# A graph layer on one core: kept messages, three slot tables, gather rows by ScalarE, and a rearranged start and end

## The chip, the cores and the metric

The kernel runs on one core of one Trainium2 chip. The metric is the device time of one execution in microseconds (us); beside it stands one execution recorded by the hardware profiler, with a span from its first to its last instruction. The core has TensorE (PE, matrix products), VectorE (DVE), ScalarE (ACT), GpSimd (POOL) and SyncE (SP), which here only starts DMA transfers. Each engine takes its instructions in order, so an instruction that waits holds up all that is queued behind it on its engine.

## The reference, cut to what matters

```python
# x [12500,128]; 400000 edges, sorted by dst; src random; src is the row that is added to
h   = relu(layernorm(x)) @ W_in2f.T
Wij = (smu(edge_attr_20 @ W_f1.T + b_f1) @ W_f2.T + b_f2) * edge_weight[:, None]
agg = segment_sum(h[dst] * Wij, src, 12500)          # rows gathered at dst, summed at src
out = x + (smu(agg @ W_o1.T + b_o1) @ W_o2.T + b_o2)
# smu(x) = ((1+a)x + (1-a) x erf(mu (1-a) x)) / 2, written as a gelu plus a linear part
```

## The kernel before, in words

Edges are taken in tiles of 128; four tiles are a group (782 groups, the unit of the main loop) and two groups a supergroup (391). The sum over `src`, which is in random order, is made by sorting messages into bins. A bin is 128 nodes (98 bins). A run of supergroups is an epoch, and each epoch has a table `buf{k}` in DRAM with a fixed number of slots for each bin. A message takes the next free slot of its bin: POOL writes it there with one scatter, an indirect DMA of 128 rows of 129 numbers, for every tile (L649). When an epoch is over, its table is read back bin by bin and added up on TensorE while the next epoch's messages are made.

One group goes through these steps; the numbers are lines of the profile:

- `load` (SP): edge attributes `f` (L439), target positions `rbc` broadcast to all partitions (L449), and a window of 42 rows of h (L463);
- `hide`, `bend`, `smooth`: first filter product on TensorE (`pu`, L563), gelu on ScalarE (L571), linear part on VectorE (L579);
- `pick`: 0/1 gather rows `oh` by VectorE, once for a supergroup (L472);
- `gather`, `take`: rows of h by a product with `oh` (`ph`, L597), copied by ScalarE (L605);
- `weigh`, `mix`: second filter product (`pw`, L616), times the gathered rows on VectorE (`mt`, L626);
- `bins`, `count`, `read`, `number`: the slot of every message (VectorE L497, TensorE L511 to L514, VectorE L541 and L550);
- `turn`: the message times w_o1, which also turns edges onto partitions (`pt`, TensorE, L636);
- `send`: ScalarE scales by the edge weight into an `ms` tile (L643, L646), and POOL scatters it.

The steps of several groups are interleaved by hand; each engine gets its instructions in the order of the program. POOL's scatters come only from `send`, and there are six `ms` tiles, so that ScalarE can be at most six groups ahead of POOL. The main loop is, in its order (before.py, L938 to L958):

```python
            if g:
                turn(g)
                send(g)
            ...
            number(g + 1); weigh(g + 1); gather(g + 1); take(g + 1)
            parts(k - 1, lo + (hi - lo) // 2)      # half of this group's adds
            mix(g + 1)
            ...
            hide(g + 2); bend(g + 2); count(g + 2); smooth(g + 2)
            if g % PER == 0:
                pick((g + 4) // PER)
            bins(g + 3)
            read(g + 2)
            parts(k - 1, hi)                       # the other half
```

`parts` adds up the epoch before: `fetch` reads table rows on SP's queue (L680), `choose` makes 0/1 rows by comparing each row's node number (L691, VectorE), `add` multiplies both on TensorE into `pg` (L704), and VectorE adds `pg` into `agg` (L717, L715 for the first epoch). `begin` and the first `choose` of an epoch stand in its second and third group: they wait for the last scatter of the epoch before, and VectorE waits with them.

Tables are cleared with zeros beforehand by DMAs on SP's queue (`clear`, L179), as slots stay empty. In the first epoch the rows of h are made between the steps (`rows_of_h`: L205 normalizes on ScalarE). Near the end of the last epoch rows of x come in for the output (`old_rows`), and POOL adds the output bias to them (`with_bias`, L250). After the last scatter, the last table is added up, and for every four bins gelu (L994, ScalarE), a sum (L1000, POOL), the product with w_o2 (L264) and the store follow.

At the very start POOL fills four buffers and a block of zeros, loads weights and clears the last bin's rows, before its first scatter (L393 to L411).

Of the kernel before, what the change touches and what calls it, by code (L numbers as in the profile page):

```python
# [31 lines left out]
PARTS = (59, 59, 59, 59, 48, 37, 27, 27, 16)  # L32
# [8 lines left out]
def gnn_kernel(  # L41
# [46 lines left out]
    for a, n in eps_of:  # L88
        mean = n * SUP * P * P / N
        dev = SIGMA * math.sqrt(mean)  # L90
        CAP.append(math.ceil((mean + dev) / P) * P)
        ZMIN.append(max(0, math.floor((mean - dev) / ZP) * ZP))
# [10 lines left out]
    bufs = [dram.tile([NB * CAP[k], ROW], F32, name=f"buf{k}") for k in range(EPOCHS)]  # L103
# [17 lines left out]
    nc.vector.tensor_add(prow, prow, late)  # L121
    irow = const.tile([P, P], F32, name="irow")
# [5 lines left out]
    nc.vector.tensor_scalar(lift, ident, BIG, None, op0=ALU.mult)  # L128
    nc.vector.scalar_tensor_tensor(tri, irow, pcol, lift, op0=ALU.is_gt, op1=ALU.add)
    ones_h = const.tile([P, P], F16, name="ones_h")  # L130
    nc.vector.memset(ones_h, 1.0)
    rest_h = const.tile([P, P], F16, name="rest_h")
    nc.vector.tensor_sub(rest_h, ones_h, tri)
    none = const.tile([P, NB], F16, name="none")
    nc.vector.memset(none, 0.0)
# [6 lines left out]
    b1w = const.tile([P, P], F32, name="b1w")  # L142
# [14 lines left out]
    b2row = const.tile([1, P], F32, name="b2row")  # L157
    b1 = const.tile([P, 1], F32, name="b1")
    bz = const.tile([P, 1], F32, name="bz")
    w_o1 = const.tile([P, P], F32, name="w_o1")  # L160
# [4 lines left out]
    zero = const.tile([ZP, CB * max(c - z for c, z in zip(CAP, ZMIN)) * ROW // ZP], F32, name="zero")  # L165
# [69 lines left out]
    units = [(b, n, P) for b, n in chunks(NB - 1, GRP)] + [(NB - 1, 1, LASTB)]  # L235
# [39 lines left out]
    with tc.tile_pool(name="ld", bufs=4) as ld, \  # L275
# [8 lines left out]
        irow_ps = ps1.tile([P, GRP * P], F32, name="irow_ps")[:, 0:P]  # L284
        nc.vector.tensor_copy(irow_ps, irow)
# [106 lines left out]
        fill(0, nc.vector)  # L392
        nc.gpsimd.memset(w_f1, 0.0)  # L393
        nc.gpsimd.dma_start(w_f1[0:R, :], w_f1_t)
        nc.gpsimd.dma_start(w_f1[R:R + 1, :], b_f1)
        nc.sync.dma_start(fbufs[0][0:R, :], f_t[:, 0:SUP * P])
        nc.scalar.dma_start(w_o1, w_o1_t)
        nc.scalar.dma_start(x_sb[:, 1:HEAD, :], bin_rows(x, 1, HEAD - 1))
        nc.gpsimd.dma_start(w_f2, w_f2_t)
        nc.gpsimd.dma_start(b2, b_f2.rearrange("o p -> p o"))  # L400
        one["fetched"]()
        nc.gpsimd.dma_start(w_sb[:, 0:CH], w_col[:, 0:CH])
        fill(1, nc.gpsimd)
        nc.gpsimd.memset(zero, 0.0)
# [390 lines left out]
        for s in (1, 2):  # L795
            load(s)
# [397 lines left out]
```

## Time and profile before

| | |
|---|---|
| time, median of 3 runs | 4111.01 us (4106.05 to 4113.0) |
| the profiled execution: time; span | 4114.52 us; 4112.7 us |
| mean granted TensorE clock | 0.976 |
| busy: TensorE, VectorE, ScalarE, POOL | 3675.1, 3450.5, 1944.9, 3096.4 us |
| DMA | 820.83 MB, mean 200 GB/s |
| chain that ended last, by engine | PE 39%, DVE 29%, DMA 18%, ACT 6%, issue 5%, POOL 2% |

How to read it: a row of a group shows line, engine, operation, output and inputs with the count, then busy time and mean duration of one in ns, then the engine's idle time just before them and what ended most of it. "Issue" is idle time in which the engine waited for nothing that the profile shows. Rows of the timeline start with the start and duration in us. Rows of the windows begin with the stretch and its length, then busy time and count of the engines in the order PE, PEld (weight loads), DVE, ACT, POOL (or of the one engine asked for), then granted clock, DMA share and GB/s. A TensorE product in float32 shows as two passes, a transpose as one.

### The profile page before, as it was taken

What the parts mean: (1) busy time and instruction counts of PE and PEld (TensorE: products, weight loads), DVE (VectorE), ACT (ScalarE), POOL (GpSimd) and SP (SyncE); (2) the same over time, 40 slices, a digit from 0 to 9 for tenths busy, and PEclk for the clock granted to TensorE, in tenths of its full rate; (3) what the DMA queues carried; (4) which work ended last, traced back from release to release, by engine and by line L of the source; (5) the groups of instructions that cost most, each with busy time, mean ns of one, the idle gap of its engine ahead of it and who ended that gap; (6) DMA issues with size and microseconds to landing.
All of it is one profiled execution on the core that took longest, in us unless ns stands there. A gap on an engine that the chain in (4) does not pass through costs nothing.

```text
span 4112.7 us, 74065 instructions
## 1 busy us (share of the span) xinstructions
PE 3675.1 (89%) x21113; PEld 2552.3 (62%) x21117; DVE 3450.5 (84%) x7657; ACT 1944.9 (47%) x5690; POOL 3096.4 (75%) x3199
## 2 busy tenths in 40 slices
PE   7878887999888998979999979999899989999898
PEld 4445545666655666646666656666677767666678
DVE  8988776888878888868888868888799979888897
ACT  4457754444444444435444434444444434444442
POOL 6777777777777777777777777777777777777775
PEclk9999998999999999989999989999999999999999
DMA  6866656766647666646766647777688789887668
GB/s 187 231 187 182 191 166 183 213 202 195 188 141 219 198 201 197 199 146 196 212 199 187 199 148 207 210 204 211 176 228 223 195 230 242 221 228 221 176 195 248
DMA packets 564245, 820.83 MB, mean 200 GB/s; under 512 B 178033, under 2 KB 378488, under 8 KB 563698
## 3 DMA queue, kind: packets, MB, share of 16 engines
q1 hardware_dynamic: 456096, 604.98, 53.5%
q0 software_dynamic: 100320, 207.40, 15.7%
q10 hardware_dynamic: 7410, 3.65, 0.3%
q8 instruction: 167, 2.74, 0.3%
q14 instruction: 252, 2.06, 0.2%
HBM read 442.34 MB, written 373.37 MB: 198 GB/s over the span
## 4 chain that ended last, share of the span: by engine, by line
PE 39%; DVE 29%; DMA 18%; ACT 6%; issue 5%; POOL 2%; DVEq 0%; ACTq 0%; POOLq 0%; SPq 0%
DMA buf<-ms,ix 17%; PE pt L636 11%; PE pg L704 9%; PE pw L616 8%; DVE se L691 8%; PE pu L563 7%; DVE mt L626 5%; DVE so L497 5%; DVE sm L579 3%; DVE sl L541 3%; ACT ge L571 2%; ACT ms L646 2%; PE ph L597 2%; POOL buf L649 2%; DVE agg L717 1%
## 5 line engine op out<-in xcount | busy, mean ns | idle before, releaser
L649 POOL DMA_INDIRECT buf<-ms,ix x3125 | 3025.4, 968 | 972.7 <-issue 395.9
L646 ACT ACTIVATE ms<-pt,w_sb 128x128 f32<-128x128 f32 x3125 | 888.8, 368 | 1125.5 <-PE pt L636 1118.0
L636 PE MATMUL pt<-w_o,mt 128*128 128x128 f32 x6250 | 881.3, 284 | 390.9 <-DVE mt L626 388.4
L704 PEld LDWEIGHTS pg<-se,rw 128*128 128x128 f32 x8036 | 1052.4, 192 | 249.7 <-issue 210.8
L704 PE MATMUL pg<-se,rw 128*128 128x128 f32 x8036 | 1148.8, 280 | 4.5 <-DVE se L691 3.7
L636 PEld LDWEIGHTS pt<-w_o,mt 128*128 128x128 f32 x6250 | 765.5, 193 | 478.7 <-DVE mt L626 474.5
L497 DVE SCALAR_TENSOR_TENSOR so<-irow_ps,hi_f,so 128x98 f16<-128x98 f32 x3116 | 989.0, 317 | 82.7
L616 PE MATMUL pw<-sm,w_f 128*128 128x512 f32 x1564 | 826.7, 611 | 10.4 <-DVE sm L579 8.5
L563 PE MATMUL pu<-f,w_f 128*128 128x512 f32 x1564 | 811.4, 601 | 0.0
L626 DVE SCALAR_TENSOR_TENSOR mt<-pw,b,hg 128x512 f32<-128x512 f32 x782 | 583.6, 746 | 207.3 <-ACT hg L605 203.8
L571 ACT ACTIVATE ge<-pu 128x512 f32<-128x512 f32 x782 | 468.6, 599 | 532.7 <-PE pu L563 526.5
L579 DVE SCALAR_TENSOR_TENSOR sm<-pu,ge 128x512 f32<-128x512 f32 x782 | 535.3, 684 | 187.8 <-ACT ge L571 182.0
L691 DVE TENSOR_TENSOR se<-irow_ps,rw 128x1536 f32<-128x1536 f32 (+1 forms) x345 | 587.9, 1704 | 114.3 <-DMA rw<-buf 110.2
L605 ACT ACTIVATE hg<-ph 128x512 f32<-128x512 f32 x782 | 468.6, 599 | 62.1 <-PE ph L597 44.9
L541 DVE TENSOR_REDUCE sl<-pc 128x4 f32<-128x392 f32 x782 | 434.7, 556 | 0.0
L643 ACT ACTIVATE ms<-lo_b 128x4 f32<-128x4 bf16 x782 | 159.9, 204 | 358.7 <-DMA buf<-ms,ix 358.2
L597 PE MATMUL ph<-oh,hw 126*128 126x512 bf16 x770 | 298.3, 387 | 0.0
L563 PEld LDWEIGHTS pu<-f,w_f 128*128 128x128 f32 x1564 | 253.5, 196 | 53.4 <-issue 43.8
L511 PE MATMUL pc<-so,tri 128*128 128x392 f16 x782 | 257.9, 330 | 1.0 <-DVE sl L541 0.8
L616 PEld LDWEIGHTS pw<-sm,w_f 128*128 128x128 f32 x1564 | 241.1, 195 | 24.7 <-DVE sm L579 21.4
L513 PEld LDWEIGHTS <-rest_h 128*128 128x128 f16 x781 | 76.5, 98 | 265.9 <-issue 265.9
L513 PE MATMUL pc<-so,rest_h 128*128 128x294 f16 x781 | 225.1, 288 | 0.0
(161 smaller groups left out, 1391.0 us busy)
## 6 DMA issues: line engine op xcount, KB each, us to landing
rw<-buf SPq DMA_DIRECT2D x292, 774.0 KB
rbc<-rel_dram SPq DMA_DIRECT2D x389, 256.0 KB
buf<-zero SPq DMA_DIRECT2D x243, 387.0 KB
buf<-ms,ix POOLq DMA_INDIRECT x3125
buf<-zero SPq DMA_DIRECT2D x193, 258.0 KB
rw<-buf SPq DMA_DIRECT2D x49, 645.0 KB
f<-in_f_t SPq DMA_DIRECT2D x390, 80.0 KB
hw<-h_dram SPq DMA_DIRECT2D x770, 31.5 KB
```

The costliest lines, as they stand in the source:

```text
L497: nc.vector.scalar_tensor_tensor(so[:, j], irow_ps[:, :NB], hi_f[:, t + j:t + j + 1], so[:, j - 1] if j else before, op0=ALU.is_equal, op1 ...
L541: nc.vector.tensor_reduce(sl[:, :n], pc[:, :n], op=ALU.max, axis=AX.X)
L563: nc.tensor.matmul(pu[:, :n], w_f1, loaded[g // PER][0][:, o:o + n], start=True, stop=True)
L571: nc.scalar.activation(ge[:, :n], units_of[g][:, :n], AF.Gelu, scale=ZS)
L579: nc.vector.scalar_tensor_tensor(sm[:, :n], units_of.pop(g)[:, :n], LIN, hidden[g][:, :n], op0=ALU.mult, op1=ALU.add)
L616: nc.tensor.matmul(pw[:, :n], w_f2, hidden.pop(g)[:, :n], start=True, stop=True)
L626: nc.vector.scalar_tensor_tensor(mt[:, :n], pws.pop(g)[:, :n], b2, rows_of.pop(g)[:, :n], op0=ALU.add, op1=ALU.mult)
L636: nc.tensor.matmul(pt[:, j, :], mt[:, j * P:(j + 1) * P], w_o1, start=True, stop=True)
L646: nc.scalar.activation(ms[:, j, 0:P], pt[:, j], AF.Copy, scale=w_sb[:, t + j:t + j + 1])
L649: i = nc.gpsimd.indirect_dma_start(out=bufs[k][:, :], out_offset=bass.IndirectOffsetOnAxis(ap=ix[:, j:j + 1], axis=0), in_=ms[:, j, :], in ...
L691: nc.vector.tensor_tensor(se[:, :m], irow_ps.unsqueeze(1).to_broadcast([P, m, P]), rows_in[c][:, :m, P:P + 1].to_broadcast([P, m, P]), op= ...
L704: nc.tensor.matmul(pgs[0][:, g, :], rows_in[c][:, o, 0:P], sel[c][:, o, :], start=(q == 0), stop=(q == Q[k] - 1))
```

## The change

Six edits are made together.

1. **Kept messages.** The last supergroups form two smaller epochs (16 and 7; the epochs are now 59, 59, 59, 59, 48, 37, 27, 20, 16, 7). Their 23 supergroups are computed early, one after every nine from supergroup 67 on; their messages go to DRAM and are read back and scattered after all others, while the adds of the epochs before go on.
2. **The product with w_o1** is left out of `turn` for all messages but the kept ones: `turn` is a plain transpose, and `agg` is multiplied once by w_o1 (`fold`), when the last such epoch has been added up.
3. **Three tables** serve all ten epochs in turn. A message carries its node number plus 128 for each time its table has been used, so that old rows match nothing; only the first three epochs are cleared.
4. **Gather rows by ScalarE in two passes**, relu(1 - |target - row|), a group at a time; VectorE still makes them for the first six supergroups.
5. **The start**: weight loads from SP's queue in place of POOL's; VectorE takes a second fill; POOL's other fills wait for VectorE, which touches each buffer after its first `bins`; the counting constants come later.
6. **The end**: rows of x and their bias (now on VectorE) come beside the kept scatters; the first large `choose` of the last table is made in three pieces, and the last full unit of four bins is split in two.

The core of the diff:

```diff
-PARTS = (59, 59, 59, 59, 48, 37, 27, 27, 16)
+PARTS = (59, 59, 59, 59, 48, 37, 27, 20, 16, 7)
+SENT_LAST = 2
+BUFS = 3
-    bufs = [dram.tile([NB * CAP[k], ROW], F32, name=f"buf{k}") for k in range(EPOCHS)]
+    stores = [dram.tile([NB * CAP[k], ROW], F32, name=f"buf{k}") for k in range(min(BUFS, EPOCHS))]
+    bufs = [stores[k % BUFS][0:NB * CAP[k], :] for k in range(EPOCHS)]
...
         fill(0, nc.vector)
+        fill(1, nc.vector)
...
-        nc.gpsimd.dma_start(w_f1[0:R, :], w_f1_t)
-        nc.gpsimd.dma_start(w_f1[R:R + 1, :], b_f1)
+        nc.sync.dma_start(w_f1[0:R, :], w_f1_t)
+        nc.sync.dma_start(w_f1[R:R + 1, :], b_f1)
...
+        def quiet_ends():                      # called after product(), counting_constants(), bins(0)
+            for t in (zero, fbufs[2], zr, fbufs[3], x_sb[:, NB - 1, :]):
+                nc.vector.memset(t[:, 0:2], 0.0)
+            nc.gpsimd.memset(zero, 0.0)
+            clear(0, len(cleans) - 1, nc.gpsimd)
+            fill(2, nc.gpsimd)
+            nc.gpsimd.memset(zr, 0.0)
+            nc.gpsimd.dma_start(h_dram[NB * P:N + P, :], zr[:N + P - NB * P, :])
+            fill(3, nc.gpsimd)
+            nc.gpsimd.memset(x_sb[:, NB - 1, :], 0.0)
...
+        flow, rest_of = [], list(range(EARLY, NS))      # EARLY = 368
+        start, gap = eps_of[1][0], (eps_of[5][0] - eps_of[1][0]) // (NS - EARLY)
+        for s in range(EARLY):
+            flow.append(s)
+            if s >= start and (s - start) % gap == gap - 1 and rest_of:
+                flow.append(rest_of.pop(0))
...
+        def pick_part(g):
...
+            nc.scalar.activation(oh, loaded[s][1][:, o:o + n], AF.Abs, bias=nrow)
+            nc.scalar.activation(oh, oh, AF.Relu, scale=-1.0, bias=onesb[:, 0:1])
...
         def turn(g):
...
-                nc.tensor.matmul(pt[:, j, :], mt[:, j * P:(j + 1) * P], w_o1, start=True, stop=True)
+                if s_of(g) < EARLY:
+                    nc.tensor.transpose(pt[:, j, :], mt[:, j * P:(j + 1) * P], ident)
+                else:
+                    nc.tensor.matmul(pt[:, j, :], mt[:, j * P:(j + 1) * P], w_o1, start=True, stop=True)
...
         def send(g):
...
+            m = epoch[s_of(g)] // BUFS
+            if m:
+                nc.scalar.activation(ms[:, :n, P], lo_b[:, t:t + n], AF.Identity, bias=mark[:, m:m + 1])
...
+            if s_of(g) >= EARLY:
+                nc.scalar.dma_start(kept_rows[:, t - kept_tile:t - kept_tile + n, :], ms[:, :n, :])
+                return
+            scatter(g, ms)
...
+        def fold():
+            dst = plain.pop(0)
+            w = dst.shape[1]
+            po = ps1.tile([P, GRP * P], F32, name=("pu", "ph")[len(folded) % 2])
+            nc.tensor.matmul(po[:, :w], w_o1, dst, start=True, stop=True)
+            nc.scalar.activation(dst, po[:, :w], AF.Copy)
...
-            if g % PER == 0:
-                pick((g + 4) // PER)
+            pick_part(at(p + 4))               # at(p): the group at place p of the new order
...
+        def refill(g):
+            if g < NG:
+                t, n = groups[g]
+                back[g] = msg.tile([P, GRP, ROW], F32, name="ms")
+                nc.sync.dma_start(back[g][:, :n, :], kept_rows[:, t - kept_tile:t - kept_tile + n, :])
+
+        g1 = EARLY * PER
+        for g in range(g1, g1 + 4):
+            refill(g)
+        for g in range(g1, NG):
+            refill(g + 4)
+            k = chores(g)                      # clears, begin, choose, share of the adds
+            scatter(g, back.pop(g))
+            parts(k - 1, hi)
+            if g - g1 >= 2:
+                old(g - g1 - 2)                # rows of x, SP's queue
+            biased(g - g1 - 10)                # with_bias on VectorE
```

The kept groups have no share of the adds; `LEFT`, 36 adds of the last but one table, is still kept back for the time after the last group.

More of the change, by code (lines that the diff above doesn't have):

```diff
@@ L91, in gnn_kernel @@
         CAP.append(math.ceil((mean + dev) / P) * P)
-        ZMIN.append(max(0, math.floor((mean - dev) / ZP) * ZP))
+        ZMIN.append(max(0, math.floor((mean - dev) / ZP) * ZP) if len(ZMIN) < BUFS else 0)
+    assert all(c <= CAP[k % BUFS] for k, c in enumerate(CAP)) and (EPOCHS - 1) // BUFS < GRP
     Q = [c // P for c in CAP]
```

259 lines of the change are left out of this document (157 added, 102 removed).

## The prediction

> **What bounds the kernel now.** I read the page first: busy times, then the costliest groups.
>
> ```profile
> span 4112.7 us, 74065 instructions
> PE 3675.1 (89%) x21113; PEld 2552.3 (62%) x21117; DVE 3450.5 (84%) x7657; ACT 1944.9 (47%) x5690; POOL 3096.4 (75%) x3199
> L649 POOL DMA_INDIRECT buf<-ms,ix x3125 | 3025.4, 968 | 972.7 <-issue 395.9
> ```
>
> TensorE (PE) looks like the bound and GpSimd (POOL) like an engine with a quarter to spare. But the 972.7 us that POOL stood idle before its 3125 scatters are 0.31 us each, mostly "issue": it waited for nothing. So I read POOL's own timeline.
>
> ```profile
> 19.93 1.04 POOL L649 DMA_INDIRECT buf<-ms,ix  x1 [10.27 <-ACT ms L646]
> ...
> 1499.61 0.96 POOL L649 DMA_INDIRECT buf<-ms,ix  x1 [0.30 <-issue]
> 1500.88 0.96 POOL L649 DMA_INDIRECT buf<-ms,ix  x1 [0.30 <-DVE ix L550]
> 1502.14 0.96 POOL L649 DMA_INDIRECT buf<-ms,ix  x1 [0.30 <-DMA buf<-ms,ix]
> ...
> 4022.18 0.96 POOL L649 DMA_INDIRECT buf<-ms,ix  x1 [0.30 <-issue]
> ```
>
> A scatter starts every 1.265 us (1499.61 to 1502.14, two steps), 0.96 busy and a fixed 0.30 whatever releaser is named. The 3124 steps from first to last take at least 3124 x 1.265 = 3951.9 us; they took 4022.18 - 19.93 = 4002.3. POOL is saturated from 20 to 4022 us. The span is 19.9 (head) + 3951.9 + 50.4 (excess) + 90.5 (after the last scatter). No edit here changes the number of scatters, so only head, excess and tail can shrink; time taken from TensorE or VectorE (DVE) in between buys nothing by itself.
>
> The excess: 3125 x (0.968 - 0.96) = 25 us is scatters that ran long; about 14 us is POOL's bias adds (below); some 12 us is left for scatters that came late.
>
> **The production rate.** Messages queue before POOL in six `ms` tiles. After each table change VectorE sits out POOL's whole backlog, then the engines refill the queue at their own rate:
>
> ```profile
> 641.77 1.76 DVE L691 TENSOR_TENSOR se<-irow_ps,rw 128x1536 f32<-128x1536 f32 x1 [20.46 <-DMA rw<-buf]
> 649.10:906.90 257.80, 40.33 (x54) 1.00 0.69 203
> 649.10:906.90 257.80, 242.81 (x1415) 169.67 (x1414) 226.40 (x493) 128.16 (x379) 195.97 (x204) 1.00 0.69 203
> ```
>
> The second line counts the `mt` products of L626: 54 groups in 257.8 us, 4.77 us a group against POOL's 4 x 1.265 = 5.06. The third (columns PE, PEld, DVE, ACT, POOL) gives per group TensorE 4.50, VectorE 4.19, ScalarE (ACT) 2.37: TensorE sets that rate, 94% busy.
>
> **The change part by part.**
>
> ```profile
> L636 PE MATMUL pt<-w_o,mt 128*128 128x128 f32 x6250 | 881.3, 284 | 390.9 <-DVE mt L626 388.4
> L211 PE MATMUL pg<-ident,rw 128*128 128x128 f32 x97 | 16.2, 283 | 0.8 <-ACT rw L205 0.6
> L472 DVE TENSOR_SCALAR oh<-rbc,prow 128x1024 bf16<-128x1024 bf16 x384 | 200.3, 522 | 0.0
> L605 ACT ACTIVATE hg<-ph 128x512 f32<-128x512 f32 x781 | 468.3, 600 | 62.1 <-PE ph L597 44.9 <-PE ph L595 16.5
> L994 ACT ACTIVATE ge<-agg,bz 128x512 f32<-128x512 f32 x24 | 17.0, 721 | 52.2 <-DVE ms L268 22.1 <-POOL hg L250 16.8 <-DVE agg L717 7.2
> ```
>
> *Transposes for the product with w_o1.* Two passes a tile (881.3/3125 = 0.28 us) become one (16.2/97 = 0.17): 0.46 us a group less on TensorE. The product is made up by 24 folds of 512 columns in the last phase, where TensorE has room. Gain on the path: none, but production speeds up.
>
> *Gather rows by ScalarE.* VectorE loses 0.26 us a group (200.3/768 groups). ScalarE gains two passes over 512 elements with a per-partition bias; bounds 0.60 (L605) and 0.72 (L994, from SBUF with such a bias), and I take 0.70, as it is nearer in kind: 1.4 us a group, the second pass waiting for the first. Queued behind them on ScalarE is the next group's `send`, which POOL waits for. ScalarE then has 2.37 + 1.4 = 3.8 us, less than 4.55 (below).
>
> The Trainium skill ("ScalarE: Activation LUTs", What ACT_TABLE_LOAD costs) gives 280 ns + 0.833 ns an element for a pointer bias, an estimate of 707 ns a pass; the sum would be the same. Its rule for kernel authors there, to use VectorE and not ScalarE for relu-like work, speaks against this edit.
>
> On POOL the pick's removal is a real gain:
>
> ```profile
> 1512.08 0.48 DVE L472 TENSOR_SCALAR oh<-rbc,prow 128x1024 bf16<-128x1024 bf16 x1
> 1512.27 1.12 POOL L649 DMA_INDIRECT buf<-ms,ix  x1 [0.30 <-issue]
> ```
>
> The scatter beside the pick took 1.12 instead of 0.96. Going through all 3125 in the timeline, 118 of the 139 scatters above 0.99 us overlap a pick (one in ten of the others does), and those beside picks hold 18 of the 24-25 us. Gain 18 us, at least 0 if the lengthening has another cause. By the Trainium skill ("SBUF — State Buffer", Who interferes with whom) such a VectorE instruction locks GpSimd out for its whole length: by that, 384 x 0.48 = 184 us would go. The trace has the effect, but only a tenth of the size, since 25 us is all the lengthening there is.
>
> *Bias adds from POOL to VectorE.*
>
> ```profile
> 3874.65 0.96 POOL L649 DMA_INDIRECT buf<-ms,ix  x1 [0.30 <-issue]
> 3875.63 2.50 POOL L250 TENSOR_TENSOR w_sb<-w_sb,bo 128x512 f32<-128x512 f32 x2
> 3878.30 0.98 POOL L649 DMA_INDIRECT buf<-ms,ix  x1 [0.17 <-issue]
> ...
> L250 POOL TENSOR_TENSOR w_sb<-w_sb,bo 128x512 f32<-128x512 f32 x5 | 6.4, 1283 | 0.1
> L250 POOL TENSOR_TENSOR hi_f<-hi_f,bo 128x512 f32<-128x512 f32 x5 | 6.3, 1276 | 0.1
> L250 POOL TENSOR_TENSOR lo_b<-lo_b,bo 128x512 f32<-128x512 f32 x2 | 2.6, 1283 | 0.0
> ```
>
> Two adds stretched a step from 1.265 to 3.65, 1.2 each; twelve lie between scatters: 14 us gone. On VectorE they fall in the last phase, where it has room.
>
> *Kept messages, smaller last tables.* 23 of 391 supergroups are computed early, their messages written to DRAM by ScalarE's queue (46 DMAs, each waiting for the stores just before it, with the next group's `take` behind it), and scattered after everything else. In the stretch where they are slipped in, 20 computed groups feed POOL 18 groups' scatters, so production must hold 18 x 5.06 / 20 = 4.55 us a group. I expect about 4.3: TensorE has 4.50 - 0.46 = 4.04, at today's 94% 4.3. Cost 0, if it holds. Just after a table change the queue is short: a pair of kept groups takes about 8.6 us against a few us of backlog, and at supergroups 121 and 238 a pair comes 3 to 4 supergroups after a change. I put down 5 us, bounds 0 and 15.
>
> In the last phase POOL has 181 scatters, about 229 us, with only adds, loads and folds beside it: 98 x (3 + 2) - 36 = 454 adds of 0.25 (from the row of L704 below, 48.26 us for 192) are 114 us of TensorE. POOL goes on at 1.265 if its messages come back in time; SP reloads four groups ahead, 20 us. An epoch of 7 supergroups adds 98 adds (25 us of TensorE) and 9 choosings to the kernel, hidden there.
>
> *Three tables in turn.* Two thirds of the zero fills on SP's queue go. POOL was never late for them in the middle of the run, so 0. Marks are ScalarE adds in place of copies, 0.
>
> *After the last scatter.*
>
> ```profile
> 4031.55 1.76 DVE L691 TENSOR_TENSOR se<-irow_ps,rw 128x1536 f32<-128x1536 f32 x1 [1.46 <-DMA rw<-buf]
> 4031.50:4102.10 70.60, 48.26 (x384) 46.19 (x384) 0.98 0.94 283
> 4031.50:4102.10 70.60, 23.86 (x175) 21.37 (x176) 0.98 0.94 283
> L717 DVE TENSOR_TENSOR agg<-agg,pg 128x512 f32<-128x512 f32 x192 | 130.8, 681 | 25.0 <-PE pg L704 24.7
> L691 DVE TENSOR_TENSOR se<-irow_ps,rw 128x1536 f32<-128x1536 f32 x292 | 511.3, 1751 | 103.3 <-DMA rw<-buf 100.1 <-PE pg L704 2.7
> ```
>
> 9.4 us pass before the last table's rows are there; then TensorE runs without a break, 48.3 us for the adds (L704) and 23.9 for the products with w_o2 (L264); 10.6 us end it. The last table now has one row block a bin, not two: 24 + 24 = 48 us on TensorE. VectorE has 9 x 1.75 + 25 x 2 x 0.68 = 50 us, so it sets 51. With halves and pieces saving about 2 us at the ends, 9 + 51 + 9.5 = 69.5 instead of 90.5: 21 us gained (14 to 26).
>
> *Head.*
>
> ```profile
> 3.90 5.12 DVE L305 CAST ssf<-ss 128x48 f32<-128x48 int32 x1
> 4.62 0.97 POOL L291 MEMSET f<- 128x1024 f32 x1
> 14.40 0.29 DVE L223 TENSOR_TENSOR rw<-ph,h_first 128x128 f32<-128x128 f32 x1
> ```
>
> A small cast took 5.1 us while POOL filled memory; POOL's fills now come behind VectorE's first sums, so VectorE runs ahead. It also takes a second fill, and the counting constants come just before the sums, so 2 to 3 us of the 5 are left, and POOL's fills (some 4.5 us in its queue ahead of the first scatter, waiting for VectorE) then lie where the first messages are made, after the point that stood at 14.40. I take 2 us (from +1, if `other_parts` is held up as the cast was, to -4). Five weight loads go from POOL to SP's queue ahead of two column loads, about 2 us later there; nobody in the first group waits for those: 0.
>
> *Sum.* -18 - 14 - 21 - 2, one late step at a table change (2 us) no longer late, +5 for kept pairs, +1 for the late rows of the first epoch: -51. The profiled execution took 4114.5 (span 4112.7 and 1.8 around it) and gives 4063; it is 3.5 above the median of 4111, which gives 4060.
>
> **The rivals.**
>
> *ScalarE makes production too slow; slower than before.* If the second pass, its wait and the message writes leave production at today's 4.77, each cycle of 20 groups takes 95.4 us against POOL's 91.1; 23 cycles lose 99 us: 4160. The point of decision is 4.55, where loss begins, and 4.66 a group, where it eats the 51 us. For it: each group's `take` waits behind `send` and the passes of the group before, so a chain through ScalarE replaces TensorE's. Against it: ScalarE 3.8, VectorE 3.9, TensorE 4.0 all lie well below. Chance 0.18.
>
> *Late rows.* In 320 to 480 us the rows of h run too:
>
> ```profile
> 320.00:480.00 160.00, 139.32 (x721) 86.94 (x720) 131.87 (x317) 123.40 (x346) 122.23 (x125) 1.00 0.66 192
> 3300.00:3600.00 300.00, 284.65 (x1729) 206.62 (x1730) 265.44 (x556) 135.43 (x400) 226.18 (x235) 0.98 0.90 237
> 4035.00:4101.00 66.00, 62.65 (x544) 61.58 (x543) 52.91 (x61) 16.30 (x23) 40.14 (x33) 0.99 0.93 280
> ```
>
> ScalarE has 123.4/31.6 = 3.9 us a group; with 1.4 more, 5.3 > 5.06. Over some 50 groups that is 12 us, which six tiles (25 us) can hold if full. If the passes cost 0.72 with full waits and the queue is short, 20 us are lost: 4080. Chance 0.1.
>
> *The last phase is bound by DMA.* Scatters and reloads 12 MB each, table rows 32, rows of x 6: 62 MB in 229 us are 271 GB/s. The stage from 3300 moved 237 at 0.90 share with POOL at 1.277 a scatter, the one from 4035 moved 280. At 237 the phase takes 262 us: 33 lost, 4093. Chance 0.1.
>
> **How the numbers follow.** The forecast, POOL's steps and the four gains, has 0.62, with its own range from 4040 to 4078. The two middle rivals have 0.2 and end faster, save where both meet (0.03, near no change). The first rival has 0.18, of which 0.01 lies near no change. A measurement can tell 0.2%, 8 us. So faster 0.79, same 0.04, slower 0.17. The range goes from 4035, all gains at their upper ends, to 4105, past the middle rivals, and leaves out the first.
>
> **What would show it.** Right: scatters at 1.265 with a mean of about 0.962; first start near 18 us, last near 3991; no POOL add among them; after the last, about 70 us. Wrong: gaps of several us on POOL from 700 to 1900 with ScalarE's passes just ahead (first rival), between 320 and 560 (second), or steps above 1.3 in the last 230 us of scattering with a DMA share near 1 (third). A first scatter above 20 us would show the head's gain lost.

## The result, and the profile after

The changed kernel takes 4065.58 us (median of 5 runs, 4062.12 to 4068.08), the kernel before 4108.48 (5 runs, 4104.56 to 4113.0) on the same chip: ratio 0.9895, 95% interval 0.988 to 0.9909. The forecast was 4060, with a range from 4035 to 4105. The profiled execution took 4063.85 us, its span is 4062.1.

Seven of the twelve runs below met chips on which the kernel before took 4975 to 5100 us at a mean granted TensorE clock of 0.91 to 0.93, and kernels with the change ran at 0.87 to 0.89; they are compared only with each other and with the kernel before in the same state, called "the low clock" here.

The page of the changed kernel, busy times and POOL's main group:

```profile
span 4062.1 us, 69847 instructions
...
PE 3492.8 (86%) x18417; PEld 2246.9 (55%) x18420; DVE 3328.4 (82%) x7355; ACT 2962.7 (73%) x7256; POOL 3042.2 (75%) x3168
...
L726 POOL DMA_INDIRECT buf<-ms,ix x2944 | 2829.0, 961 | 916.0 <-issue 270.6
```

TensorE lost 182 us of work and VectorE 122, ScalarE gained 1018, yet the time moved by 1%. The scatters' mean fell from 968 to 961 ns. POOL's timeline shows where the 50.6 us of span came from (start and duration first):

```profile
19.42 1.05 POOL L726 DMA_INDIRECT buf<-ms,ix  x1 [3.59 <-ACT ge L633]
...
3989.89 0.96 POOL L726 DMA_INDIRECT buf<-ms,ix_kept  x1 [0.30 <-issue]
3991.16 0.96 POOL L726 DMA_INDIRECT buf<-ms,ix_kept  x1 [0.30 <-issue]
```

The first scatter comes 0.5 us earlier than before (19.93), the last at 3991.16 and not at 4022.18, and 70.9 us follow it in place of 90.5. POOL is still saturated: 3971.7 us for 3124 steps, 1.271 each. I took the steps apart in the same way for both kernels: a scatter that overlaps a pick and its excess over 0.96 ("lengthening"), idle time above the fixed 0.30 ("gaps"), and the plain steps that are left.

| us of the span | before | after | difference | forecast |
|---|---|---|---|---|
| ahead of the first scatter | 19.9 | 19.4 | -0.5 | -2 |
| lengthening beside picks | 18.0 | 0.6 | -17.4 | -18 |
| gaps: bias adds on POOL | 14.2 | 0 | -14.2 | -14 |
| gaps: late messages, kept groups | 0 | 10.5 | +10.5 | +5 |
| gaps: other late messages | 12.1 | 5.2 | -6.9 | -2 +1 |
| plain steps | 3957.9 | 3955.4 | -2.5 | 0 |
| after the last scatter | 90.5 | 70.9 | -19.6 | -21 |
| sum | 4112.7 | 4062.1 | -50.6 | -51 |

The sums belong to two single executions. The one before took 6.0 us more than the median of that kernel's five runs and the one after 1.7 less, so the medians differ by 42.9 us and not by 50.6.

Production, in a stretch where kept groups are slipped in (all engines in the first row, the `mt` products alone in the second):

```profile
1272.00:1805.00 533.00, 491.69 (x2585) 313.26 (x2585) 466.54 (x1028) 432.40 (x1072) 404.50 (x422) 1.00 0.59 170
...
1272.00:1805.00 533.00, 89.26 (x120) 1.00 0.59 170
```

120 groups in 533 us are 4.44 us a group, under the 4.55 that POOL needs; TensorE is busy for 92% of it. Behind the table change at supergroup 236 it is not under it (two cycles of 20 groups, the same two views):

```profile
2447.20:2635.10 187.90, 174.79 (x957) 114.96 (x956) 164.83 (x351) 148.69 (x360) 137.95 (x145) 1.00 0.62 182
...
2447.20:2635.10 187.90, 29.86 (x40) 1.00 0.62 182
```

40 groups in 187.9 us are 4.70 us a group. This epoch has only 48 supergroups in which to add up the table of 59: 460 passes of adds (L787) fall on these 40 groups, where 372 fall on the 40 from 1346.5 to 1525.4 us, and TensorE is busy for 4.37 us a group in place of 4.12, which is the likely reason. 9.0 of the 10.5 us of gaps at kept groups lie here, at three kept pairs one after another, and only 1.4 behind the table change at supergroup 118; the cycle after these two, at 4.53 us a group, lost nothing. The first of the three:

```profile
2446.44 0.96 POOL L726 DMA_INDIRECT buf<-ms,ix  x1 [0.30 <-issue]
2450.78 0.96 POOL L726 DMA_INDIRECT buf<-ms,ix  x1 [3.38 <-ACT ms L715]
```

The step is 4.34 us and not 1.265: POOL waits for ScalarE's `ms`, because a kept pair was computed in between.

The stretch behind the last scatter in the windows, first of the kernel before, then of the changed one:

```profile
4023.00:4112.00 89.00, 75.44 (x644) 73.78 (x643) 63.96 (x75) 17.68 (x26) 46.89 (x41) 0.96 0.85 258
```

```profile
3992.00:4062.00 70.00, 54.22 (x461) 52.05 (x460) 52.43 (x74) 18.29 (x27) 31.66 (x28) 0.95 0.70 192
```

TensorE and VectorE are busy for 54 and 52 us there, in place of 75 and 64, and the first large `choose`, in three pieces, comes 10.0 us after the last scatter (VectorE's timeline):

```profile
4001.20 1.89 DVE L771 TENSOR_TENSOR se<-irow_ps,rw 128x512 f32<-128x512 f32 x3 [0.41 <-DMA rw<-buf]
```

### The profile page after: what moved, and what is told of

Read it like the earlier page. It is cut to its first block, busy times and chain, and to the rows that moved or that the text cites. A ratio compares the mean times of both kernels' runs of the same rounds, so it can differ in the third digit from the quotient of the medians.

```text
span 4062.1 us, 69847 instructions
## 1 busy us (share of the span) xinstructions
PE 3492.8 (86%) x18417; PEld 2246.9 (55%) x18420; DVE 3328.4 (82%) x7355; ACT 2962.7 (73%) x7256; POOL 3042.2 (75%) x3168
## 2 busy tenths in 40 slices
DMA packets 510392, 759.72 MB, mean 187 GB/s; under 512 B 174949, under 2 KB 313462, under 8 KB 509856
## 3 DMA queue, kind: packets, MB, share of 16 engines
q0 software_dynamic: 100112, 207.06, 15.3%
## 4 chain that ended last, share of the span: by engine, by line
PE 41%; DVE 26%; DMA 13%; ACT 9%; issue 6%; POOL 4%; ACTq 0%; SPq 0%; DVEq 0%; POOLq 0%
PE pw L678 13%; DMA buf<-ms,ix 10%; PE pg L787 10%; DVE se L771 9%; PE pu L625 7%; PE pt L699 7%; DVE mt L688 5%; POOL buf L726 4%; DVE sl L600 3%; ACT ms L715 3%; ACT ge L633 2%; DVE sm L641 2%; PE ph L659 2%; DVE so L556 2%; DVE agg L800 2%
## 5 line engine op out<-in xcount | busy, mean ns | idle before, releaser
L726 POOL DMA_INDIRECT buf<-ms,ix x2944 | 2829.0, 961 | 916.0 <-issue 270.6
L787 PEld LDWEIGHTS pg<-se,rw 128*128 128x128 f32 x8232 | 1080.8, 194 | 343.3 <-issue 277.1
L787 PE MATMUL pg<-se,rw 128*128 128x128 f32 x8232 | 1175.7, 282 | 96.4 <-DVE se L771 75.1
L556 DVE SCALAR_TENSOR_TENSOR so<-irow_ps,hi_f,so 128x98 f16<-128x98 f32 x2936 | 929.7, 317 | 78.0
L678 PE MATMUL pw<-sm,w_f 128*128 128x512 f32 x1564 | 884.1, 648 | 47.9 <-DVE sm L641 46.9
L771 DVE TENSOR_TENSOR se<-irow_ps,rw 128x1536 f32<-128x1536 f32 (+2 forms) x356 | 602.3, 1692 | 229.5 <-DMA rw<-buf 228.3
L699 PE MATMUL pt<-ident,mt 128*128 128x128 f32 x2944 | 468.9, 282 | 362.7 <-DVE mt L688 361.1
L699 PEld LDWEIGHTS pt<-ident,mt 128*128 128x128 f32 x2944 | 327.6, 142 | 447.2 <-DVE mt L688 444.4
L524 ACT ACTIVATE oh<-oh,onesb 128x512 bf16<-128x512 bf16 x770 | 555.5, 721 | 25.2
L523 ACT ACTIVATE oh<-rbc,nrow 128x512 bf16<-128x512 bf16 x770 | 551.2, 716 | 1.2 <-DMA rbc<-rel_dram 1.2
```

Source lines behind the costliest of these rows:

```text
L524: nc.scalar.activation(oh, oh, AF.Relu, scale=-1.0, bias=onesb[:, 0:1])
L556: nc.vector.scalar_tensor_tensor(so[:, j], irow_ps[:, :NB], hi_f[:, t + j:t + j + 1], so[:, j - 1] if j else before, op0=ALU.is_equal, op1 ...
L678: nc.tensor.matmul(pw[:, :n], w_f2, hidden.pop(g)[:, :n], start=True, stop=True)
L699: nc.tensor.transpose(pt[:, j, :], mt[:, j * P:(j + 1) * P], ident)
L726: i = nc.gpsimd.indirect_dma_start(out=bufs[k][:, :], out_offset=bass.IndirectOffsetOnAxis(ap=ix[:, j:j + 1], axis=0), in_=ms[:, j, :], in ...
L771: nc.vector.tensor_tensor(se[:, a:a + n], own.unsqueeze(1).to_broadcast([P, n, P]), rows_in[c][:, a:a + n, P:P + 1].to_broadcast([P, n, P] ...
```

## The experiments

**Picks by VectorE again, a group at a time.**

```diff
-            nc.scalar.activation(oh, loaded[s][1][:, o:o + n], AF.Abs, bias=nrow)
-            nc.scalar.activation(oh, oh, AF.Relu, scale=-1.0, bias=onesb[:, 0:1])
+            nc.vector.tensor_scalar(oh, loaded[s][1][:, o:o + n], prow, None, op0=ALU.is_equal)
```

> The changed kernel with the 0/1 gather rows made by VectorE again (one is_equal over 512 columns a group, in bf16) in place of ScalarE's two passes; nothing else differs. Theory (POOL sets the time, and VectorE's picks lengthen the scatters beside them): some 736 picks lengthen scatters again by 18 to 20 us in all, first and last scatter otherwise as in the changed kernel, so about 4085 us, 20 us slower. Rival (ScalarE's two passes slow production, and their removal is worth half of what the picks cost): the gaps after the table changes (10 us) go as well, so about 4075 us. Second rival (the lengthening had another cause): under 4067 us, mean scatter still 0.961.

4084.64 us (4 runs, 4080.14 to 4091.58), ratio to the kernel before 0.9949 [0.9932, 0.9966]: 19 us slower than the changed kernel, as the theory had it, and for another reason. Its page, the last scatter in POOL's timeline, and the same two windows as above:

```profile
L725 POOL DMA_INDIRECT buf<-ms,ix x2944 | 2827.9, 961 | 936.7 <-issue 372.9
```

```profile
4009.71 0.96 POOL L725 DMA_INDIRECT buf<-ms,ix_kept  x1 [0.30 <-issue]
```

```profile
1272.00:1805.00 533.00, 479.45 (x2522) 305.59 (x2521) 483.55 (x1114) 281.28 (x812) 400.38 (x418) 1.00 0.56 167
...
1272.00:1805.00 533.00, 86.57 (x117) 1.00 0.56 167
```

The scatters' mean stayed at 961 ns, and only 2.9 us of lengthening in all lie beside 770 picks. The gaps grew instead, from 15.7 to 35.4 us: 117 groups in 533 us are 4.56 a group, just past 4.55, and VectorE, with its picks of 0.36 us, is now as busy (483.6) as TensorE (479.5). So here ScalarE's passes are worth 19 us through production, and the theory of the lengthening looked dead. The timelines show why these picks don't lengthen (VectorE's pick and the scatter that starts while it runs):

```profile
475.32 0.35 DVE L523 TENSOR_SCALAR oh<-rbc,prow 128x512 bf16<-128x512 bf16 x1
475.41 1.08 POOL L725 DMA_INDIRECT buf<-ms,ix  x1 [0.30 <-issue]
...
1521.31 0.96 POOL L725 DMA_INDIRECT buf<-ms,ix  x1 [0.30 <-ACT ms L711]
1521.80 0.56 DVE L523 TENSOR_SCALAR oh<-rbc,prow 128x512 bf16<-128x512 bf16 x1
```

A scatter is lengthened when a pick began in the pause ahead of it and still runs some 0.13 us into it: 475.67 - 475.41 = 0.26, lengthened by 0.12. A pick that begins half a microsecond into a scatter is itself held (0.56 in place of 0.34), and the scatter is not. I sorted all picks by how long after a scatter's start they began. In the kernel before 90 of 392 began 1.0 to 1.2 us after it, and 15.3 us of excess lie with them; all others together hold less than 3. Here 119 of 777 began there, with 3.6 us (the scatters beside the other picks lie a little under 0.96): a pick of 0.34 reaches much less far into the next scatter than one of 0.48.

**Whole-supergroup picks by VectorE**, to test that reading.

```diff
-            s, i = divmod(g, PER)
-            if s < FEW // SUP: ...          # else ScalarE's two passes
+            s, i = divmod(g, PER)
+            if i == 0:
+                pick(s)                     # is_equal over 1024 columns, VectorE
```

> The changed kernel with the 0/1 gather rows made by VectorE as in the kernel before: one is_equal over 1024 columns for two groups, in place of ScalarE's passes. In the kernel before, 90 of 392 such picks began 1.0 to 1.2 us after the start of a scatter and lengthened the next one by 0.17 us each (15.3 us); with 512 columns (run e1_pick_dve) 119 of 777 picks that began there cost 0.03 each (3.6 us). Theory (what counts is a long pick that still runs when the next scatter begins): the lengthening comes back, 14 to 16 us, with 80 to 90 lengthened by 0.17; VectorE's load is 0.26 us a group and not 0.36, so the gaps at the table changes grow by less than the 20 us of e1_pick_dve, by some 10; together about 4090 us. Rival (the lengthening in the kernel before came from something else that is gone, such as the zero fills or the bias adds): scatter mean stays 0.961, about 4076 us from the gaps alone.

It ran at the low clock: 5220.52 us (4 runs), the kernel before 5082.55, ratio 1.0277 [1.0221, 1.0334]. The time says nothing of the theory, since POOL isn't saturated there, but the rows do:

```profile
1293.81 0.48 DVE L507 TENSOR_SCALAR oh<-rbc,prow 128x1024 bf16<-128x1024 bf16 x1
...
1293.98 1.13 POOL L718 DMA_INDIRECT buf<-ms,ix  x1 [0.30 <-issue]
```

The pick ends 0.31 us into the scatter, which takes 0.17 longer. 107 picks that began 1.0 to 1.2 us after a scatter's start hold 11.9 us; scatters beside picks hold 14.0 us in all, against 2.9 with the short picks. So in a kernel with the change's tables and bias adds the lengthening is back once the picks are long: it is the picks, by their length and their phase. What it costs in time at the full clock wasn't measured.

**The product with w_o1 in every group.**

```diff
-                if s_of(g) < EARLY:
-                    nc.tensor.transpose(pt[:, j, :], mt[:, j * P:(j + 1) * P], ident)
-                else: ...
+                nc.tensor.matmul(pt[:, j, :], mt[:, j * P:(j + 1) * P], w_o1, start=True, stop=True)
...                                          # and no fold()
```

> The changed kernel with the product with w_o1 made in every group in place of the turn (two passes a tile in place of one on TensorE, 0.28 us a tile for 0.16), and without the folds at the end of the main part. Theory (production must keep under 4.55 us a group where kept groups are slipped in): TensorE gets 4 x 0.12 = 0.49 us more a group, production goes from about 4.45 to 4.8-4.9, each cycle of 20 groups takes 96 to 98 us against POOL's 91.1, 23 cycles lose 110 to 160 us less the backlog and the cycles in which ScalarE is the slower; between 60 and 130 us slower, 4125 to 4195. Rival (POOL alone sets the time, production has room): within 5 us of the changed kernel, 4060 to 4070, as 25 us of TensorE in folds go.

4107.35 us (10 runs, 4106.73 to 4111.48), ratio 0.9999 [0.9989, 1.0009]: 42 us slower than the changed kernel, the whole gain gone by one edit undone. Less than the theory's 60, and the mechanism is its own (windows, then POOL's timeline):

```profile
1272.00:1805.00 533.00, 504.02 (x2911) 348.84 (x2910) 451.52 (x986) 419.37 (x1032) 395.58 (x412) 1.00 0.55 167
...
1272.00:1805.00 533.00, 85.91 (x115) 1.00 0.55 167
```

```profile
1179.66 0.96 POOL L723 DMA_INDIRECT buf<-ms,ix  x1 [0.30 <-issue]
1182.41 0.96 POOL L723 DMA_INDIRECT buf<-ms,ix  x1 [1.78 <-ACT ms L712]
...
4036.36 0.96 POOL L723 DMA_INDIRECT buf<-ms,ix_kept  x1 [0.31 <-issue]
```

115 groups in 533 us, 4.63 a group, TensorE busy for 95%. Gaps such as that at 1179.66 (1.5 us) come once in each cycle of 20 groups, every 93.0 us from 900 to 1644: POOL's 91.1 and the 2 that production lacks. Gaps are 60.2 us in all for 15.7, and the last scatter comes 45 later. The mis-sized step was the rate: I had added 0.49 us of TensorE work a group to 4.45 nearly in full; TensorE's busy time a group rose by 0.29 in this window and the time of a group by 0.2. The gaps are not all alike, though: 22 of the 60 us lie behind the table change at supergroup 236.

**Two row blocks in the last table.**

```diff
-        CAP.append(math.ceil((mean + dev) / P) * P)
+        CAP.append(max(2 * P, math.ceil((mean + dev) / P) * P))   # and begin(k) behind the parts
```

> The changed kernel with two row blocks a bin in the last table in place of one (its size not below 256), and its first piece begun only after all its parts are listed. Theory (what follows the last scatter is bound by TensorE and VectorE and grows with the row blocks): last scatter at 3991 us as before, then 92 us in place of 70.9, so about 4086 us, 21 us slower. Rival (that stretch is bound by the DMA of the table's rows, whose number is little changed): under 6 us slower, 4071 at most.

4083.73 us (4 runs, 4078.41 to 4085.46), ratio 0.9937 [0.992, 0.9953]: 18 us slower than the changed kernel. Its last scatter, and the window behind it:

```profile
3997.19 0.96 POOL L726 DMA_INDIRECT buf<-ms,ix_kept  x1 [0.30 <-issue]
```

```profile
3998.00:4083.00 85.00, 75.96 (x669) 74.95 (x668) 67.32 (x83) 18.28 (x27) 31.87 (x28) 0.97 0.80 240
```

86.5 us follow the last scatter in place of 70.9, with 22 more of TensorE and 15 more of VectorE. The first large `choose` of that table comes 11 us after the last scatter in place of 10, as it is begun later. So some 15 us, three quarters of the tail's gain, are the smaller last table. The run doesn't separate the engines' work from the DMA of the rows, since a table with two blocks also has twice the rows (the windows show 240 GB/s in place of 192). The other 6 us of the profiled execution are a later last scatter, from gaps (21.0 in place of 15.7), which I can't put down to the edit.

**Only the bias adds moved, in the kernel before.**

```diff
-                with_bias(unit, xr, nc.gpsimd)
+                with_bias(unit, xr, nc.vector)
```

> The kernel before with one edit: the bias adds of x by VectorE and not by POOL. Theory (POOL is saturated, each add between scatters costs its 1.2 us): twelve adds, 14.2 us, so 4094 us, ratio to the kernel before 0.9966. Rival (the last groups wait for VectorE, which is 88% busy there, or POOL had room): no change, 4108 us.

Neither: 4147.12 us (4 runs, 4141.17 to 4149.04), ratio 1.0097 [1.008, 1.0114], 39 us slower. The last scatter and two of VectorE's rows behind it in the timeline, then a row of the groups from 4004 us to the end:

```profile
4004.18 0.96 POOL L649 DMA_INDIRECT buf<-ms,ix  x1 [0.30 <-issue]
...
4058.25 0.69 DVE L250 TENSOR_TENSOR hg<-hg,bo 128x512 f32<-128x512 f32 x1 [3.50 <-DMA hg<-in_x]
4058.86 0.68 DVE L717 TENSOR_TENSOR agg<-agg,pg 128x512 f32<-128x512 f32 x1
```

```profile
L250 DVE TENSOR_TENSOR hg<-hg,bo 128x512 f32<-128x512 f32 x12 | 8.3, 691 | 42.3 <-DMA hg<-in_x 42.3
```

POOL's part behaved as forecast: the nine gaps of 14.2 us are gone, though 6 us of small ones took their place, and the last scatter came 18 us earlier than in the first profile of the kernel before, 6.5 earlier than in the second (below). But the adds took a wait along. In this kernel the other twelve full adds, which lie behind the last scatter, follow straight on the load of their rows; on POOL most of that wait was hidden (9.3 us at its row of 12 adds), while on VectorE the adds and the `agg` sums of the last table queue behind it: 42.3 us of waiting, and 135 us after the last scatter in place of 90.5. The changed kernel loads these rows eight groups ahead into places of their own, and there the move cost nothing.

**The bias adds on POOL, in the changed kernel** (run twice, both at the low clock).

```diff
-                with_bias(*rows_got[n], nc.vector)
+                with_bias(*rows_got[n], nc.gpsimd)
```

> The changed kernel with the 25 bias adds of x by POOL again, in the last phase between the scatters, and not by VectorE. Theory (POOL is saturated to the last scatter): 25 adds, 24 of them 1.2 to 1.28 us, move the last scatter from 3991 to about 4021 us, the rest behind it stays at 69 to 71: about 4095 us, 30 us slower. Rival (in the last phase POOL waits for DMA or VectorE anyway, so that adds lie in idle time): under 10 us slower.

> Once more the changed kernel with the 25 bias adds of x by POOL, in the last phase between the scatters. Theory (POOL is saturated to the last scatter): the last phase of 181 scatters takes 231 + 30 = 261 us, the last scatter comes at 4021, the time is about 4095 us where the kernel before takes 4108. Rival (POOL has idle time in the last phase for the adds): under 10 us slower than the changed kernel.

5287.32 us beside 5082.55 for the kernel before (1.0405 [1.0336, 1.0474]), and 5222.57 beside 5024.33 (1.0404 [1.0363, 1.0444]). The last phase of 181 scatters took 278 and 283 us with the adds in it, and 282 to 311 without them (the five other runs at the low clock): where POOL waits, 30 us of adds are free. It doesn't test the theory, which is about a saturated POOL; for that stand the nine gaps of the kernel before and their absence in the run ahead of this.

**Kept groups away from the table changes, last bin cleared first**, meant as a version that beats both.

```diff
+        places_kept = {66, 74, 82, 90, 98, 106, 114, 126, 134, 142, 150, 158, 166, 173,
+                       185, 193, 201, 209, 217, 225, 232, 248, 262}
-            if s >= start and (s - start) % gap == gap - 1 and rest_of:
+            if s in places_kept:
...
+        nc.gpsimd.memset(zero, 0.0)          # at the start of POOL's queue,
+        clear(0, len(cleans) - 1, nc.gpsimd) # and no longer in quiet_ends()
```

> The changed kernel with two edits: the 23 kept supergroups are slipped in at places that lie away from the table changes (every 8 supergroups or so, none within four behind a change) in place of every 10th; and the zero memset with the clearing of the last bin stands at the start of POOL's queue again, ahead of the fills that wait for VectorE. Theory: in the changed kernel the gaps behind the two table changes that meet kept groups were 1.4 and 9.0 us, and the first scatter waited until 19.42 us for the zero fill issued at 13.03; so the gaps fall to 2 or less (8 to 9 us gained), the first scatter comes at 17.4 (2 us): about 4055 us on a chip where the kernel before takes 4108, ratio 0.987. Rival (with cycles of 8 to 9 supergroups production must hold 4.5 us a group, which it does not, and small gaps come at every kept pair): 4060 to 4075. Second rival for the first scatter: it waits for something else, and stays at 19.4. Where TensorE's granted clock is so low that production and not POOL sets the time (0.88 and 5083 us for the kernel before in the four runs ahead of this one), neither edit changes anything.

> Once more the changed kernel with the kept supergroups placed away from the table changes and the last bin cleared first. Theory, where POOL sets the time (the kernel before near 4108 us): first scatter at 17.7 as in e9_both, gaps behind the table changes at most 2 us in place of 10, so 4055 us, ratio 0.987 to the kernel before, 10 less than the changed kernel's 4065.6. Rival (every cycle of 8 to 9 supergroups now starves POOL a little, since production at 4.44 us a group leaves no more than 0.06 us a group there): 4062 to 4075. Where the granted clock is near 0.88 and production sets the time: some 4% slower than the kernel before, as the last phase of 181 scatters follows behind production instead of beside it.

Both runs met the low clock: 5219.06 us, 1.0412 [1.0374, 1.0451], and 5202.21, 1.0392 [1.0362, 1.0422]. So whether it is faster at the full clock stays open. Its start can be read, since POOL's first 20 us hardly depend on production:

```profile
1.69 0.73 POOL L411 MEMSET zero<- 128x774 f32 x1
2.74 0.77 POOL L187 DMA_DIRECT2D buf<-zero  x1 [0.32 <-POOL zero L411]
...
17.41 1.05 POOL L728 DMA_INDIRECT buf<-ms,ix  x1 [3.00 <-ACT ms L717]
```

First scatter at 17.41 and 17.73 us; the other kernels with the change had it at 19.2 to 20.2. That was the lost head gain.

**Kept groups after every 4th supergroup, and ten tables in place of three.**

```diff
-        start, gap = eps_of[1][0], (eps_of[5][0] - eps_of[1][0]) // (NS - EARLY)
+        start, gap = eps_of[1][0], 4
...
-BUFS = 3                                     # the other kernel
+BUFS = 10
```

> The changed kernel with the 23 kept supergroups slipped in after every 4th supergroup in place of every 10th. In a cycle 10 groups are computed while 8 are scattered (8 x 5.06 = 40.5 us), so production would have to hold 4.05 us a group. Theory (production there is 4.45 to 4.55 us a group, and what it lacks is lost on POOL for good): 44.5 to 45.5 us a cycle, 4 to 5 us lost in each of 23, 92 to 115, less a backlog of 15: 4140 to 4165 us. Rival (the placing of the kept groups counts little, since the same number of groups is computed in all): 4060 to 4075 us.

> The changed kernel with ten slot tables in place of three in turn, so that all ten are filled with zeros and none is used again. Theory (the zero fills on SyncE's queue are late for nobody): 4065 us, within 4 either way. Rival (the fills compete with the scatters' and the rows' DMA, or hold up the loads behind them on that queue): 10 us slower or more.

Both at the low clock, beside 5082.55 for the kernel before: 5314.59 us, 1.0458 [1.0401, 1.0516], and 5346.49, 1.0505 [1.0434, 1.0576]. Inconclusive for both theories. The kernel with the early kept groups lies among the others on that chip (5220 to 5346 us), which fits a POOL that waits anyway, but the changed kernel itself was not run there. The ten tables moved 863.85 MB in place of 759.72 and were the slowest of the four on that chip; whether the fills cost time at the full clock isn't known. What this state shows is the rate of production (windows, the `mt` products again; first with ten tables, then with the kept groups placed, second run):

```profile
1272.00:1805.00 533.00, 65.12 (x87) 0.89 0.50 148
```

```profile
1272.00:1805.00 533.00, 66.59 (x89) 0.90 0.45 138
...
4824.00:5125.00 301.00, 167.17 (x941) 136.96 (x942) 106.75 (x109) 14.72 (x25) 168.67 (x175) 0.71 0.61 195
```

6.1 and 6.0 us a group, over POOL's 5.06: production sets the time, and POOL idles. The third row is the last phase of the second kernel: TensorE 167 us and VectorE 107 of 301. My reading, which is argued and not shown: with production as the bound, the 181 kept scatters that used to run beside it now follow behind it (main part to 4814 us, then 294, then 88), so that the kernels with the change are 3 to 5% slower. To show it, the kernel before was run once more:

> The kernel before, unchanged, for a profile in the state in which the last seven runs found the chips: granted TensorE clock 0.87 to 0.89, the kernel before at 4975 to 5100 us, and kernels with the change some 4% slower (e9_both, e9b_both, e11b_bias_pool). Their traces show production at 6.0 us a group in the main part, the last of the non-kept scatters at 4814 to 4848, then 283 to 300 us for the 181 kept scatters and 86 to 88 us behind the last. Theory (where production sets the time, keeping messages moves 181 scatters from beside production to behind it): the kernel before produces its 782 groups at about the same rate, 6.0 to 6.3 us, its last scatter comes at 4880 to 4940 and 95 to 110 us follow, 4980 to 5040 in all, with POOL idle 1.2 to 1.6 us for most groups. Rival (the change slows production itself, by ScalarE's passes): the kernel before produces at 5.7 or less in the same stretch, 700 to 1165 and 1272 to 1805 us, where the changed one has 6.0, and more than 95 us pass behind its last scatter only if the tail is slower too. Should the chip be back at a clock of 0.97, the run shows 4108 again and tells nothing.

4103.86 us (one run, on another chip, at a clock of 0.977), so the question stays open. Two figures speak for the reading, without showing it. The kernel of e10_pick_whole, which has no passes on ScalarE, made 87 groups from 1272 to 1805 us too, though it was the least slow of the four on its chip. And with some 110 us outside the scatters, as at the full clock, the kernel before would have needed (4999.59 - 110) / 782 = 6.25 us a group on the chip of e9b_both, an estimate, where 4814 / 782 is 6.16. What no run separates is the clock itself: the kernels with the change ran at 0.87 to 0.89 in the mean and the kernel before at 0.91 to 0.93.

The run is a second look at the kernel before at the full clock (last scatter in the timeline, then the page):

```profile
4010.66 0.96 POOL L649 DMA_INDIRECT buf<-ms,ix  x1 [0.31 <-issue]
```

```profile
L649 POOL DMA_INDIRECT buf<-ms,ix x3125 | 3014.5, 965 | 972.2 <-issue 390.6
```

Lengthening beside picks is 16.5 us (18.0 in the first profile), gaps of the bias adds 14.2 (14.2), 91.4 us after the last scatter (90.5). The plain steps are 3949.7 in place of 3957.9 us. So the large terms repeat within 2 us, and terms below some 8 us in the plain steps mean nothing.

## Why the prediction was right

- **POOL is the bound.** Right. Steps stay at 1.265 us, and last scatter (3991) and the time behind it (71) came where they were put. TensorE's and VectorE's savings bought nothing by themselves, but the kept groups need them: without the transposes the whole gain goes (e2_w_o1_all), with the picks on VectorE 19 us of it (e1_pick_dve).
- **The sum, -51.** Right within some 10 us; that the profiled pair gives -50.6 is luck. The medians give -42.9, and against the second profile of the kernel before (span 4102.1, on another chip) it is -40.0, with plain steps 5.7 longer in place of 2.5 shorter. The terms of the picks, the adds and the tail stay within 2 us.
- **Picks, -18.** Measured -17.4, and shown to be the picks by run e10_pick_whole. The Trainium skill ("SBUF — State Buffer", Who interferes with whom) has GpSimd locked out for the whole length of such an instruction; the runs show less: of 205 us of picks in the kernel before 18 came back as lengthening, of 280 us in e1_pick_dve 2.9. Only picks that run across the start of a scatter counted.
- **Why that edit pays.** Half of the reason was missing. Had I moved the picks' form and not their engine, 512 columns on VectorE, nearly all of the 18 us would have gone as well, but e1_pick_dve shows that 19 us come back through production. The rule of the Trainium skill to use VectorE and not ScalarE for relu-like work ("ScalarE: Activation LUTs", Rules for kernel authors) would have lost here: ScalarE had the room and VectorE hadn't (e1_pick_dve, 19 us slower). The passes took 716 and 721 ns on the changed kernel's page, for the 700 of the forecast:

```profile
L524 ACT ACTIVATE oh<-oh,onesb 128x512 bf16<-128x512 bf16 x770 | 555.5, 721 | 25.2
L523 ACT ACTIVATE oh<-rbc,nrow 128x512 bf16<-128x512 bf16 x770 | 551.2, 716 | 1.2 <-DMA rbc<-rel_dram 1.2
```

- **Bias adds, -14.** Right in the terms and the room on VectorE; that this room depends on loads that run far ahead was not said, and e3_before_bias_dve shows that without them the move costs 39 us.
- **Production about 4.3.** Mis-sized: 4.44 in the middle of the run, 4.1 us of TensorE a group at 92% busy, where the forecast had 4.04 at 94%; the margin to 4.55 was less than half of what I thought. Behind supergroup 236 there was none for two cycles, at 4.70, where the adds of a longer epoch fall into a shorter one. The forecast took one rate for all cycles. It cost little because only four kept pairs lie in that epoch.
- **Kept groups, +5.** Mis-sized for that reason: 10.5, within the bounds of 0 and 15; 6.3 of it at the two pairs that were named and 4.1 at the next two, which had been put at nothing. Other late messages fell by 6.9 in place of 1; that the two errors cancelled is luck.
- **Head, -2.** Mis-sized: -0.5. VectorE did run ahead (the small cast takes 0.18 us in place of 5.12), and ScalarE began to write the first messages into `ms` at 17.05 in place of 19.27; POOL could have followed at 17.7, as it did at 17.41 in e9b_both, 0.66 us behind ScalarE. But what was moved included a DMA: POOL's clearing of the last bin, issued at 13.03 where the kernel with it put first issues it at 2.74, and the first scatter waits for its landing (18.55 us by the semaphore events of the trace). The prediction had counted POOL's fills and not the transfer behind them (POOL's timeline of the changed kernel):

```profile
11.45 0.74 POOL L426 MEMSET zero<- 128x774 f32 x1 [9.71 <-DVE agg L425]
...
13.03 0.77 POOL L187 DMA_DIRECT2D buf<-zero  x1
```

- **Tail, -21.** Measured -19.6; e4_last_two_blocks gives some 15 of it to the one row block.
- **Rivals.** None came at the full clock: the late rows of the first epoch cost nothing, and the last phase took 231 us for 181 scatters at 1.278. The first rival's rule was borne out by e2_w_o1_all: at 4.63 to 4.65 us a group each cycle of the middle of the run lost about 2 us, and the whole change was level with the kernel before, where 4.66 had been given as the point at which the gain is eaten. It named the wrong engine (TensorE and VectorE are the near ones, not ScalarE) and the right number.

## What to carry to other kernels

Where one engine is saturated, cost a change by that engine's own timeline (first start, last start, steps that ran long, gaps), and for the others only ask whether they still deliver at the rate that it needs; then say how far the rate is from that line, and in every stage, since here 0.2 us a group was the whole gain and two cycles fell short by 0.15. When a step moves to another engine or place, its waits and its DMAs move with it: a bias add took 42 us of waiting to VectorE, and a moved fill held the first scatter. A run that gives the forecast number isn't yet the forecast cause: e1_pick_dve did so to the microsecond with another mechanism.

## What the runs showed of the hardware that was not expected

- A scatter by POOL and a bf16 comparison by VectorE hold each other up only at certain phases: a scatter is lengthened if the pick began in the pause ahead of it and runs past some 0.13 us after its start (0.17 us in the mean by picks of 0.48 in the kernel before, at most 0.12 by those of 0.34 in e1_pick_dve), and a pick is lengthened (0.34 to 0.56) if it begins half a microsecond into a scatter. Elsewhere the overlaps cost next to nothing.
- The same chip ran the kernel before in 4108 us and, later, in 5000, at a mean granted clock of 0.98 and 0.92. The kernels profiled beside it (e1_pick_dve, e9b_both) had 0.97 and 0.89, and production at 4.6 and 6.0 us a group. TensorE's busy time a group rose from 4.1 to 4.6 us there, less than the time of a group; the rest is waiting whose cause stays open. In that state POOL idles, and variants of the changed kernel lose 3 to 5% where the change wins 1% at the full clock; the changed kernel itself was not run there.
